# A four-layer graph attention stack: weight loads on GpSimd's queue, weight products moved, and other DMA latencies in the plan

## Chip, cores and metric

The kernel runs on one core of one Trainium2 chip. The metric is the device time of one execution in microseconds (us). A core has TensorE (PE: matmuls into PSUM; its weight loads are listed apart as PEld), VectorE (DVE), ScalarE (ACT), GpSimd (POOL) and SyncE (SP), which here does nothing but issue DMAs. ScalarE and GpSimd can issue DMAs too.

## The reference

128 graphs of 128 nodes with 512 features pass four layers. Each layer is a graph attention with a residual and a layer norm:

```python
x = _layernorm(x + _L0_gnn_ref(x, adj, ...))      # one head, no projection, bias b0
x = _layernorm(x + _L1_gnn_ref(adj, x, ...))      # two GAT layers: 4 heads of 256 (elu), then one of 512
x = _layernorm(x + _L2_gnn_ref(x, adj, W, a1, a2))  # 8 heads of 64
x = _layernorm(x + _L3_gnn_ref(x, adj, W_fc, W_attn))  # one head, scores from W_fc, elu
```

Every attention is of one form: two scores per node (source and target) are added over all pairs, go through a leaky relu with slope 0.2, are masked by the adjacency, and a softmax of them mixes the node features. Scores are products of projected features and attention vectors, so `x @ W @ a`; all is float32.

## The kernel before

**One graph.** A graph is one tile of 128 nodes by 512 features. The function `graph(g)` lists its operations in the order of the layers, each with an engine and a cost in us that the author gave it. The pieces that return:

- `score` (L491): products of the features with a score vector on VectorE (layers 0 and 3).
- `spread` (L326 to L333): turns a score column into a row. VectorE transposes it, one DMA on SP writes it to DRAM (`row<-sT`), a second reads it back to all 128 partitions (`w<-row`). This pair of DMAs is the "spread pair"; `nh` is the number of heads.
- `attend`: leaky relu on ScalarE (L383), mask and row minimum on VectorE (L391), exponential on ScalarE (L400), reciprocal of the sum (L408), then `turned`.
- `turned` (L344 to L359): transposes a tile of 128 x 128n. VectorE transposes blocks of 32, a DMA on SP writes them to DRAM (`scr<-w`, L349), a second reads them back (`w<-scr`, L359, or L354 where `moving` is set). This is the "turned pair".
- `project` (L449): the matmuls with the layer's weights. w1a (four chunks deep, 1032 columns in three parts), w2a (eight deep, 514 columns in two parts), wha (four deep, 528 columns in two parts).
- `mixed` (L466), `block` (L536) and `heads` (L581): the attention's matmul with the features.
- `norm`: statistics on VectorE (L418, L419), the inverse root on GpSimd (L422, L423), the scaling on VectorE (L435) or ScalarE (L431).

From its input to its output, a graph goes through one input DMA and then twelve pairs one after the other: spread and turned in layer 0, turned for x1, spread and turned in the first half of layer 1, spread and turned in the second half, turned for x2, spread and turned in layer 2, spread and turned in layer 3. GpSimd also makes the masks (L477, L480).

**The plan.** `Pipeline.plan` takes the operations of one graph and gives each a time, with every engine's time taken modulo `PERIOD`. It picks the next operation by its ready time, less `URGENCY` times the longest way to the end, plus a random shift of up to `SPREAD` (from `SEED`). `LATENCY` has two numbers for each engine: what passes from the end of an operation until a later one on the same engine, or on another, may use the result. An operation's `extra` is added to it. Graph g gets these times plus g times `PERIOD`. `run` sorts all operations of all graphs by time and emits them in that order. On the chip the times mean nothing any more: every engine works through its own list in this order and starts each operation as soon as its data is there.

**The setup.** The weights and the products that are made of them are entered into the same sorted list by `at(t, ...)`, with a time t in us of the plan:

- `weights`, `rows` and `passing` load weights with DMAs from `nc.scalar` (L213, L222).
- The score columns of a projection are appended to its weights: w1a times the attention vectors a1 in 32 products (`dot`, L262), w2a times a2 in 16 (L262), wha times a3 in eight pairs of a product and a reduction (`dots`, L280 and L281). `columns` (L294) makes the two score vectors wf of layer 3.
- A buffer of `passing` has a time until which its slot is kept.

Of the kernel before, what the change touches and what calls it, by code (L numbers as in the profile page):

```python
# [16 lines left out]
P = 128  # L17
# [7 lines left out]

PERIOD = 24.4
LATENCY = {"PE": (0.0, 0.8), "DVE": (0.15, 1.4), "ACT": (0.1, 1.4), "POOL": (0.1, 1.4), "SP": (9.0, 9.0)}
URGENCY = 1.0  # L30
BANKS = 8

SEED, SPREAD = 67, 3.0


class Buf:
# [30 lines left out]
class Pipeline:  # L67
# [3 lines left out]
    def plan(self, ops):  # L71
# [28 lines left out]
        while waiting:  # L100
# [4 lines left out]
            while True:  # L105
                u = t % PERIOD
                clash = [
                    y + d - u for x, y in spans for d in (-PERIOD, 0.0, PERIOD)
                    if u < y + d - 1e-9 and x + d < u + op.cost - 1e-9
# [3 lines left out]
                t += min(clash) + 1e-9  # L113
                assert t < ready[k] + 2 * PERIOD, "the period is too short"
            spans.append((t % PERIOD, t % PERIOD + op.cost))
            times[k] = t
# [7 lines left out]
    def run(self, setup):  # L124
# [8 lines left out]
        for g, ops in enumerate(graphs):  # L133
            alive = dict(zip(dict.fromkeys(b for op in ops for b in op.bufs), names))
            for k, op in enumerate(ops):
                events.append((g * PERIOD + times[k], g, k, op))
                op.ends = [(b, g * PERIOD + until[alive[b]]) for b in op.outs]
        for t, g, k, op in sorted(events, key=lambda e: e[:3]):
# [12 lines left out]
def tile_gat_stack(  # L151
# [25 lines left out]
    nc = tc.nc  # L177
    B, N, F = x.shape
    H1, FH = a1_src.shape
    HF = H1 * FH  # L180
    H2, FO = ah1.shape
    KF = F // P
    KH = HF // P
    OUT = w_fc.shape[0]
# [21 lines left out]
    def at(t, emit, bufs=()):  # L206
        setup.append((t, emit, bufs))

    def weights(t, shape, name, *loads, step=0.0):

        tl = const.tile(shape, F32, name=name)
        for n, (part, src) in enumerate(loads):
            at(t + n * step, lambda part=part, src=src: nc.scalar.dma_start(out=part(tl), in_=src))  # L213
        return tl

    def rows(t, ap, n, name):
        return weights(t, [P, n], name, (lambda w: w, ap.partition_broadcast(P)))

    def passing(t, until, n, src=None):

        b = Buf("setup", [P, n])
        load = lambda: nc.scalar.dma_start(out=b.ap[: src.shape[0]], in_=src)  # L222
        at(t, load if src is not None else lambda: None, [(b, until)])
        return b

# [1 line left out]

    C1, C2, C3 = HF + 2 * H1, F + 2, F + 2 * H2
    flat = "h f -> (h f)"
    w0d = rows(-20, w0_dst, F, "w0d")  # L230
    w0s = rows(-20, w0_src, F, "w0s")
    b0t = rows(-20, b0, 1, "b0t")
    a1 = [passing(-20, 40, HF, a.rearrange(flat).partition_broadcast(P)) for a in (a1_src, a1_dst)]

    w1a = weights(-20, [P, KF, C1], "w1a", *(
        (lambda w, b=b: w[b::4, :, :HF], w1.rearrange("(k b a) c -> b a k c", b=4, a=32)[b])
        for b in range(4)
    ))
    b1t = weights(-20, [P, KH], "b1t", (lambda w: w, b1.rearrange("(k p) -> p k", p=P)))
    b2t = rows(-20, b2, F, "b2t")  # L240
    a2 = [passing(-20, 110, F, a.rearrange(flat).partition_broadcast(P)) for a in (a2_src, a2_dst)]
    w2a = weights(-20, [P, KH, C2], "w2a", (lambda w: w[:, :, :F], w2.rearrange("(k p) c -> p k c", p=P)))
    fc = passing(20, 220, F, w_fc)
    ac = weights(20, [OUT, 2], "ac", *(
        (lambda w, s=s: w[:, s : s + 1], w_attn[0:1, s * OUT : (s + 1) * OUT].rearrange("u o -> o u"))
        for s in range(2)
    ))
    a3 = [passing(20, 180, F, a.rearrange(flat).partition_broadcast(P)) for a in (ah2, ah1)]
    wha = weights(40, [P, KF, C3], "wha", *(
        (lambda w, b=b, k=k: w[b::4, k, :F].rearrange("p (h o) -> p h o", h=H2),  # L250
         wh.rearrange("h (k b a) o -> b k a h o", b=4, a=32)[b, k])
        for k in range(KF) for b in range(4)
    ), step=1.2)
    acb = [passing(190, 220, P) for _ in range(2)]
    wf = const.tile([P, 2, F], F32, name="wf")
    prod = [passing(-20, 180, F) for _ in range(2)]
    turn = [0]

    def dot(w, a, out):

        turn[0] ^= 1
        nc.vector.tensor_tensor_reduce(  # L262
            out=prod[turn[0]].ap[:, : a.shape[1]], in0=w, in1=a, scale=1.0, scalar=0.0, op0=ALU.mult,
            op1=ALU.add, accum_out=out,
        )

    for k in range(KF):
        for s in range(2):
            for h in range(H1):
                c, o = slice(h * FH, (h + 1) * FH), HF + s * H1 + h  # L270
                at(14 + 4 * k + 2 * s + h / 2, lambda k=k, s=s, c=c, o=o: dot(w1a[:, k, c], a1[s].ap[:, c], w1a[:, k, o : o + 1]))
    for k in range(KH):
        for s in range(2):
            at(84 + 2 * k + s, lambda k=k, s=s: dot(w2a[:, k, :F], a2[s].ap, w2a[:, k, F + s : F + s + 1]))

    def dots(k, s):

        turn[0] ^= 1
        pr = prod[turn[0]].ap
        nc.vector.tensor_mul(pr, wha[:, k, :F], a3[s].ap)  # L280
        nc.vector.tensor_reduce(  # L281
            out=wha[:, k, F + s * H2 : F + (s + 1) * H2], in_=pr.rearrange("p (h o) -> p h o", h=H2),
            op=ALU.add, axis=AX.X,
        )

    for k in range(KF):
        for s in range(2):
            at(150 + 3 * k + 1.5 * s, lambda k=k, s=s: dots(k, s))

    def columns(s):  # L290

        nc.vector.tensor_copy(acb[s].ap[:OUT], ac[:, s : s + 1].to_broadcast([OUT, P]))
        pf = psum.tile([P, 512], F32, tag="ps7", name=f"pf_{s}")
        nc.tensor.matmul(pf, lhsT=acb[s].ap[:OUT], rhs=fc.ap[:OUT], start=True, stop=True)  # L294
        nc.vector.tensor_copy(wf[:, s, :], pf)

    for s in range(2):
        at(200 + 3 * s, lambda s=s: columns(s))

    work = ctx.enter_context(tc.tile_pool(name="work", bufs=1))  # L300
    dram = ctx.enter_context(tc.tile_pool(name="dram", bufs=1, space=bass.MemoryType.DRAM))
# [8 lines left out]
    def graph(g):  # L310
# [11 lines left out]
        def spread(col, nh):  # L322


            sT, row = Buf(f"sT{nh}", [P, nh, 32]), Buf(f"row{nh}", [nh, P])
            op("DVE", 0.12 + 0.033 * nh, lambda: nc.vector.transpose(  # L326
                sT.ap, col().unsqueeze(2).to_broadcast([P, nh, 32])
            ), [col.buf], [sT])
            op("SP", 0.6, lambda: nc.sync.dma_start(
                out=row.ap.rearrange("h (b c) -> b h c", b=P // 32), in_=sT.ap[0:P:32]  # L330
            ), [sT], [row])
            db = Buf(f"db{nh}", [P, nh, P])
            op("SP", 0.4, lambda: nc.sync.dma_start(  # L333
                out=db.ap.rearrange("p h j -> p (h j)"),
                in_=row.ap.rearrange("h j -> (h j)").partition_broadcast(P),
            ), [row], [db], 0.2 * nh)
            return db

        def turned(src, n, moving=False):

            zb, scr, out = Buf(f"zb{n}", [P, 4, n, 32]), Buf(f"scr{n}", [P, n * P]), Buf(f"pt{n}", [P, n, P])
            op("DVE", 0.12 + 0.133 * n, lambda: nc.vector.transpose(  # L344
                zb.ap.rearrange("p b h c -> p h b c"),
                src.ap.rearrange("p (h b c) -> p h b c", h=n, c=32) if len(src.shape) == 2
                else src.ap.rearrange("p h (b c) -> p h b c", c=32),
            ), [src], [zb])
            op("SP", 0.4, lambda: nc.sync.dma_start(  # L349
                out=scr.ap, in_=zb.ap.rearrange("p b h c -> p (b h c)")  # L350
            ), [zb], [scr], 0.2 * n)
            flat = lambda: scr.ap.rearrange("p f -> (p f)")
            if moving:
                op("SP", 0.6, lambda: nc.sync.dma_start(  # L354
                    out=out.ap.rearrange("p h i -> p (h i)").rearrange("p (q e) -> p q e", q=4),
                    in_=flat().rearrange("(q p e) -> p q e", q=4, p=P),
                ), [scr], [out], 0.2 * n)
                return out
            op("SP", 0.65, lambda: nc.sync.dma_start(  # L359
                out=out.ap.rearrange("p h (q c) -> p h q c", q=4),  # L360
                in_=flat().rearrange("(q p h c) -> p h q c", q=4, p=P, h=n),
            ), [scr], [out], 0.3 * n)
            return out

        class Col:
# [106 lines left out]
        x0, at = Buf("x0", [P, F]), Buf("adj", [P, P], I32)  # L472
# [25 lines left out]
        db = spread(Col(sc0, 1, 1), 1)  # L498
# [23 lines left out]
        db = spread(Col(xl, HF, H1), H1)  # L522
# [38 lines left out]
        db = spread(Col(xl2, F, 1), 1)  # L561
# [10 lines left out]
        db = spread(Col(xl3, F, H2), H2)  # L572
        x3 = Buf("x3", [P, F])

        def heads(q):
# [25 lines left out]
        db = spread(Col(sc4, 1, 1), 1)  # L601
# [6 lines left out]
            out=y.ap, in0=e3.ap, scalar=-1.0, in1=r3.ap, op0=ALU.add, op1=ALU.min  # L608
# [43 lines left out]
```

## Time and profile before

| what | value |
| --- | --- |
| median of 3 runs | 3224.28 us (3223.27 to 3225.53) |
| the profiled execution | 3223.46 us, span 3221.70 us |
| PE busy | 3081.6 us (96%), 14212 matmuls |
| PEld busy | 2375.8 us (74%) |
| DVE busy | 2792.0 us (87%) |
| ACT busy | 2470.8 us (77%) |
| POOL busy | 1545.5 us (48%) |
| DMA | 600.51 MB, mean 186 GB/s; SP's queue 588.39 MB, ACT's 8.20 MB |
| mean granted TensorE clock | 0.983 |

The profile is of one execution. Its span goes from the first to the last instruction of the program; the execution's own time lies 1.76 us above it. Busy time counts overlapping instructions of an engine once. Matmuls are pipelined, and each float32 matmul of the program shows as two records. A name such as `w<-scr` means that the tile on the left was written from the one on the right; buffer numbers are left out. The views name instructions by the line of the kernel (L449) and say what ended the idle time before them. SPq and ACTq stand for the instructions with which these engines issue DMAs.

### The profile page before, as it was taken

How to read it: one execution, taken by the hardware profiler on the slowest of the kernel's cores; microseconds unless marked ns; L12 is line 12 of the kernel's file. 1: busy time of each engine (PE TensorE's matmuls, PEld its weight loads, DVE VectorE, ACT ScalarE, POOL GpSimd, SP SyncE). 2: the span in 40 equal slices, each digit the busy share in tenths (PEclk: the TensorE clock that was granted, in tenths of full speed). 3: DMA queues.
4: the chain of work that ended last, by engine and by line, in shares of the span. 5: the costliest groups of instructions: out<-in, count | busy, mean ns of one | idle time of the engine just before them, and what ended most of it. 6: DMA issues, size and time to landing. Idle time of an engine off the chain costs nothing.

```text
span 3221.7 us, 61247 instructions
## 1 busy us (share of the span) xinstructions
PE 3081.6 (96%) x14212; PEld 2375.8 (74%) x14212; DVE 2792.0 (87%) x9976; ACT 2470.8 (77%) x8961; POOL 1545.5 (48%) x2310
## 2 busy tenths in 40 slices
PE   3799999999999999999999999999999999999974
PEld 1577777777777777777777777777777777777752
DVE  5567899999998999989999899898999989998786
ACT  0457888788787887878878888788887888878875
POOL 2234454554545545455454554545545455454334
PEclk9899999999999999999999999999999999999995
DMA  5357888888888888888888888888888888888675
GB/s 157 95 128 182 188 194 200 188 201 193 195 199 189 200 194 195 199 189 201 194 193 201 189 199 195 191 202 189 198 196 193 200 189 197 198 192 194 166 166 127
DMA packets 1641212, 600.51 MB, mean 186 GB/s; under 512 B 1310449, under 2 KB 1490673, under 8 KB 1640849
## 3 DMA queue, kind: packets, MB, share of 16 engines
q1 hardware_dynamic: 1632256, 588.39, 77.8%
q10 hardware_dynamic: 8592, 8.20, 0.8%
q8 instruction: 115, 1.88, 0.3%
q14 instruction: 249, 2.03, 0.2%
HBM read 368.91 MB, written 227.48 MB: 185 GB/s over the span
## 4 chain that ended last, share of the span: by engine, by line
PE 93%; DVE 2%; DMA 2%; ACT 2%; issue 1%; POOL 0%; ACTq 0%; SPq 0%; POOLq 0%; DVEq 0%
PE ps L449 69%; PE ps L466 10%; PE ps L536 7%; PE ps L581 6%; ACT w L400 1%; DMA w<-row 0%; PE ps L502 0%; DMA w<-scr 0%; ACT w L545 0%; DVE w L391 0%; DMA w<-in_x_dram 0%; ACT w L383 0%; DMA w_-1_2_96<-in_L_gnn_att_dst_dram 0%; DVE w L491 0%; DVE w_-1_4_110 L262 0%
## 5 line engine op out<-in xcount | busy, mean ns | idle before, releaser
L449 PE MATMUL ps<-w1a,w 128*128 128x344 f32 x3072 | 919.8, 456 | 14.0 <-DVE w L509 9.1
L449 PE MATMUL ps<-w2a,w 128*128 128x257 f32 x4096 | 917.6, 381 | 1.1 <-ACT xl L457 1.1
L400 ACT ACTIVATE w<-w,nm 128x128 f32<-128x128 f32 x1920 | 746.3, 415 | 144.3 <-DVE nm L391 142.4
L449 PEld LDWEIGHTS ps<-w2a,w 128*128 128x128 f32 x4096 | 765.8, 189 | 112.1 <-ACT xl L457 3.2
L449 PEld LDWEIGHTS ps<-w1a,w 128*128 128x128 f32 x3072 | 587.7, 192 | 307.8 <-DVE w L509 10.6
L545 ACT ACTIVATE w<-ps,b1t 128x128 f32<-128x128 f32 x2048 | 573.7, 386 | 49.5 <-PE ps L536 49.5
L383 ACT ACTIVATE w<-w,xl 128x128 f32<-128x128 f32 x1664 | 541.8, 395 | 84.8 <-PE ps L466 60.6
L422 POOL TENSOR_SCALAR rd<-mv 128x1 f32<-128x1 f32 x512 | 154.5, 302 | 935.8 <-DVE mv L419 918.8
L391 DVE CUSTOM_DVE_ANT_0 w<-w,w 128x128 f32<-128x128 f32 x1920 | 586.6, 395 | 15.6 <-ACT w L383 12.1
L344 DVE STREAM_TRANSPOSE w<-w 128x512 f32<-128x512 f32 (+1 forms) x1024 | 553.4, 546 | 10.4 <-ACT w L400 6.9
L457 ACT COPY xl<-ps 128x344 f32<-128x344 f32 (+2 forms) x640 | 265.8, 415 | 338.1 <-PE ps L449 320.5
L449 PE MATMUL ps<-wha,w 128*128 128x264 f32 x2048 | 503.3, 389 | 4.4 <-DMA w<-scr 4.4
L449 PEld LDWEIGHTS ps<-wha,w 128*128 128x128 f32 x2048 | 383.5, 192 | 122.0 <-issue 62.1
L400 ACT ACTIVATION_READ_ACCUMULATOR w<-w,nm 128x1 f32 x1920 | 410.4, 214 | 0.0
L418 DVE BATCH_NORM_STATS2 st<-w 128x6 f32<-128x512 f32 x512 | 353.9, 691 | 9.6 <-POOL w L610 2.8
L423 POOL TENSOR_TENSOR rd<-rd,neghalf 128x1 f32<-128x1 f32 x512 | 289.4, 565 | 42.7
L466 PE MATMUL ps<-w,w 128*128 128x512 f32 x512 | 260.8, 627 | 44.2 <-DMA w<-scr 23.0
L581 PEld LDWEIGHTS ps<-xl,w 128*128 128x128 f32 x2048 | 272.0, 195 | 37.6 <-ACT w L605 15.3
L391 DVE DVE_READ_ACCUMULATOR2_ANT nm<- 128x1 f32 x1920 | 290.5, 151 | 0.0
L491 DVE CUSTOM_DVE_ANT_0 w<-w,wf 128x512 f32<-128x512 f32 x256 | 284.5, 1146 | 4.4
L610 POOL TENSOR_TENSOR w<-w,w 128x512 f32<-128x512 f32 x128 | 184.1, 1439 | 202.9 <-issue 165.4
L581 PE MATMUL ps<-xl,w 128*128 128x64 f32 x2048 | 261.3, 272 | 17.5 <-ACT w L605 12.1
(63 smaller groups left out, 3741.0 us busy)
## 6 DMA issues: line engine op xcount, KB each, us to landing
scr<-w SPq DMA_DIRECT2D x640, 256.0 KB
w<-scr SPq DMA_DIRECT2D x640, 256.0 KB
w<-row SPq DMA_DIRECT2D x128, 512.0 KB
w<-in_x_dram SPq DMA_DIRECT2D x128, 256.0 KB
w<-row SPq DMA_DIRECT2D x128, 256.0 KB
out_dram<-w SPq DMA_DIRECT2D x128, 256.0 KB
w<-row SPq DMA_DIRECT2D x384, 64.0 KB
scr<-w SPq DMA_DIRECT2D x384, 64.0 KB
```

Of the source, the lines that this page charges most:

```text
L344: op("DVE", 0.12 + 0.133 * n, lambda: nc.vector.transpose(zb.ap.rearrange("p b h c -> p h b c"), src.ap.rearrange("p (h b c) -> p h b c", ...
L383: nc.scalar.activation(z.ap[:, h, :], db.ap[:, h0 + h, :], AF.Prelu, bias=src(h0 + h), alpha=SLOPE)
L391: nc.vector.tensor_tensor_reduce(out=zz.ap[:, h, :].rearrange("p (b a) -> p a b", b=4), in0=z.ap[:, h, :].rearrange("p (a b) -> p a b", b= ...
L400: nc.scalar.activation(zz.ap[:, h, :], zz.ap[:, h, :], AF.Exp, bias=nm.ap[:, h : h + 1], scale=-1.0, accum_out=rs.ap[:, h : h + 1],)
L418: op("DVE", 0.6, lambda: nc.vector.bn_stats(st.ap, y.ap), [y], [st])
L423: nc.gpsimd.tensor_tensor(out=rd.ap, in0=rd.ap, in1=neghalf, op=ALU.pow)
L449: op("PE", w * 4 / 2400 + 0.006, lambda k=k: nc.tensor.matmul(px.ap[:, :w], lhsT=xT.ap[:, k, :], rhs=wa[:, k, cols], start=(k == 0), stop= ...
L457: op("ACT", 0.16 + w / 1200, lambda: nc.scalar.copy(t.ap[:, cols], px.ap[:, :w]), [px], [t])
L466: op("PE", width * 4 / 2400, lambda: nc.tensor.matmul(pa.ap[:, :width], lhsT=pt.ap[:, 0, :], rhs=xv.ap[:, :width], start=True, stop=True), ...
L491: op("DVE", 0.75, lambda: nc.vector.tensor_tensor_reduce(out=jk.ap, in0=xv.ap, in1=wv, scale=1.0, scalar=init, op0=ALU.mult, op1=ALU.add, ...
L545: nc.scalar.activation(out.ap[:, k, :], pa.ap[:, u * P : (u + 1) * P], func, bias=b1t[:, k : k + 1])
L581: op("PE", 0.225, lambda u=u, h=h: nc.tensor.matmul(pa.ap[:, u * FO : (u + 1) * FO], lhsT=pt.ap[:, u, :], rhs=xl3.ap[:, h * FO : (h + 1) * ...
```

## The change

The loads of most weights go from ScalarE's queue to GpSimd's; w0d, w0s, b0t and b1t stay on ScalarE's; the 16 loads of wha go to SP's queue, 4 us of the plan apart. w2a is loaded in four DMAs, not one. The times of the loads and of the weight products in the plan change, and so do the times for which passing buffers are kept. SP's latency in the plan goes from 9.0 to 6.0 us, and the extras of the DMAs from 0.2nh, 0.2n and 0.3n to 1.0 + 0.1nh, 1.0 and 1.5 (the reloads); that of the input and of the store to `scr` stay. `PERIOD`, `URGENCY`, `SEED` and `SPREAD` have other values.

```diff
-PERIOD = 24.4
-LATENCY = {"PE": (0.0, 0.8), "DVE": (0.15, 1.4), "ACT": (0.1, 1.4), "POOL": (0.1, 1.4), "SP": (9.0, 9.0)}
-URGENCY = 1.0
+PERIOD = 24.7
+LATENCY = {"PE": (0.0, 0.8), "DVE": (0.15, 1.4), "ACT": (0.1, 1.4), "POOL": (0.1, 1.4), "SP": (6.0, 6.0)}
+URGENCY = 0.6
 BANKS = 8
-SEED, SPREAD = 67, 3.0
+SEED, SPREAD = 62, 8.0
...
-    def weights(t, shape, name, *loads, step=0.0):
+    def weights(t, shape, name, *loads, step=0.0, by=nc.gpsimd):
...
-            at(t + n * step, lambda part=part, src=src: nc.scalar.dma_start(out=part(tl), in_=src))
+            at(t + n * step, lambda part=part, src=src: by.dma_start(out=part(tl), in_=src))
...
-        load = lambda: nc.scalar.dma_start(out=b.ap[: src.shape[0]], in_=src)
+        load = lambda: nc.gpsimd.dma_start(out=b.ap[: src.shape[0]], in_=src)
...
-    w0d = rows(-20, w0_dst, F, "w0d")
-    w0s = rows(-20, w0_src, F, "w0s")
-    b0t = rows(-20, b0, 1, "b0t")
-    a1 = [passing(-20, 40, HF, a.rearrange(flat).partition_broadcast(P)) for a in (a1_src, a1_dst)]
-    w1a = weights(-20, [P, KF, C1], "w1a", *(
+    w0d = rows(-20, w0_dst, F, "w0d", nc.scalar)
+    w0s = rows(-20, w0_src, F, "w0s", nc.scalar)
+    b0t = rows(-20, b0, 1, "b0t", nc.scalar)
+    w1a = weights(-19, [P, KF, C1], "w1a", *(
...
-    b1t = weights(-20, [P, KH], "b1t", (lambda w: w, b1.rearrange("(k p) -> p k", p=P)))
-    b2t = rows(-20, b2, F, "b2t")
-    a2 = [passing(-20, 110, F, a.rearrange(flat).partition_broadcast(P)) for a in (a2_src, a2_dst)]
-    w2a = weights(-20, [P, KH, C2], "w2a", (lambda w: w[:, :, :F], w2.rearrange("(k p) c -> p k c", p=P)))
-    fc = passing(20, 220, F, w_fc)
-    ac = weights(20, [OUT, 2], "ac", *(
+    a1 = [passing(-18, 90, HF, a.rearrange(flat).partition_broadcast(P)) for a in (a1_src, a1_dst)]
+    b1t = weights(-18, [P, KH], "b1t", (lambda w: w, b1.rearrange("(k p) -> p k", p=P)), by=nc.scalar)
+    b2t = rows(16, b2, F, "b2t")
+    w2a = weights(18, [P, KH, C2], "w2a", *(
+        (lambda w, k=k: w[:, k : k + 2, :F], w2[k * P : (k + 2) * P].rearrange("(k p) c -> p k c", p=P))
+        for k in range(0, KH, 2)
+    ))
+    a2 = [passing(20, 130, F, a.rearrange(flat).partition_broadcast(P)) for a in (a2_src, a2_dst)]
+    a3 = [passing(60, 230, F, a.rearrange(flat).partition_broadcast(P)) for a in (ah2, ah1)]
+    fc = passing(60, 270, F, w_fc)
+    ac = weights(60, [OUT, 2], "ac", *(
...
-    a3 = [passing(20, 180, F, a.rearrange(flat).partition_broadcast(P)) for a in (ah2, ah1)]
-    wha = weights(40, [P, KF, C3], "wha", *(
+    wha = weights(70, [P, KF, C3], "wha", *(
...
-    ), step=1.2)
+    ), step=4, by=nc.sync)
...
-                at(14 + 4 * k + 2 * s + h / 2, lambda k=k, s=s, c=c, o=o: dot(w1a[:, k, c], ...))
+                at((31, 33, 56, 58)[k] + s + h / 4, lambda k=k, s=s, c=c, o=o: dot(w1a[:, k, c], ...))
...
-            at(84 + 2 * k + s, lambda k=k, s=s: dot(w2a[:, k, :F], ...))
+            at(100 + 3 * k + 1.5 * s, lambda k=k, s=s: dot(w2a[:, k, :F], ...))
...
-            at(150 + 3 * k + 1.5 * s, lambda k=k, s=s: dots(k, s))
+            at(190 + 6 * k + 3 * s, lambda k=k, s=s: dots(k, s))
...
-        at(200 + 3 * s, lambda s=s: columns(s))
+        at(250 + 3 * s, lambda s=s: columns(s))
...
-            ), [row], [db], 0.2 * nh)
+            ), [row], [db], 1.0 + 0.1 * nh)
...
-                ), [scr], [out], 0.2 * n)
+                ), [scr], [out], 1.0)
...
-            ), [scr], [out], 0.3 * n)
+            ), [scr], [out], 1.5)
```

More of the change, by code (lines that the diff above doesn't have):

```diff
@@ L207, in at, with rows @@
         setup.append((t, emit, bufs))
[L209 removed]
+    def weights(t, shape, name, *loads, step=0.0, by=nc.gpsimd):
         tl = const.tile(shape, F32, name=name)
         for n, (part, src) in enumerate(loads):
[L213 removed]
+            at(t + n * step, lambda part=part, src=src: by.dma_start(out=part(tl), in_=src))
         return tl
[L216 to L217 removed]
+    def rows(t, ap, n, name, by=nc.gpsimd):
+        return weights(t, [P, n], name, (lambda w: w, ap.partition_broadcast(P)), by=by)
     def passing(t, until, n, src=None):
         b = Buf("setup", [P, n])
[L222 removed]
+        load = lambda: nc.gpsimd.dma_start(out=b.ap[: src.shape[0]], in_=src)
         at(t, load if src is not None else lambda: None, [(b, until)])
@@ L252, in tile_gat_stack @@
         for k in range(KF) for b in range(4)
-    ), step=1.2)
-    acb = [passing(190, 220, P) for _ in range(2)]
+    ), step=4, by=nc.sync)
+    acb = [passing(240, 270, P) for _ in range(2)]
     wf = const.tile([P, 2, F], F32, name="wf")
-    prod = [passing(-20, 180, F) for _ in range(2)]
+    prod = [passing(-20, 230, F) for _ in range(2)]
     turn = [0]
@@ L270, in tile_gat_stack @@
                 c, o = slice(h * FH, (h + 1) * FH), HF + s * H1 + h
-                at(14 + 4 * k + 2 * s + h / 2, lambda k=k, s=s, c=c, o=o: dot(w1a[:, k, c], a1[s].ap[:, c], w1a[:, k, o : o + 1]))
+                at((31, 33, 56, 58)[k] + s + h / 4, lambda k=k, s=s, c=c, o=o: dot(w1a[:, k, c], a1[s].ap[:, c], w1a[:, k, o : o + 1]))
     for k in range(KH):
         for s in range(2):
-            at(84 + 2 * k + s, lambda k=k, s=s: dot(w2a[:, k, :F], a2[s].ap, w2a[:, k, F + s : F + s + 1]))
+            at(100 + 3 * k + 1.5 * s, lambda k=k, s=s: dot(w2a[:, k, :F], a2[s].ap, w2a[:, k, F + s : F + s + 1]))
     def dots(k, s):
```

## The prediction

> **What bounds the kernel now.** I read the page's slices first, then the busy time by stretches, then the chain, then the timeline of the first 60 us.
>
> ```profile
> PE   3799999999999999999999999999999999999974
> PEclk9899999999999999999999999999999999999995
> ```
>
> TensorE is full in all slices but the first two and last two. The stretches give it exactly (columns: length, then busy us and count for PE, PEld, DVE, ACT, POOL, then clock, DMA share, GB/s):
>
> ```profile
> 0.00:60.00 60.00, 8.20 (x11) 2.73 (x12) 29.20 (x127) 3.97 (x10) 14.74 (x26) 1.00 0.61 176
> 60.00:100.00 40.00, 30.74 (x78) 17.17 (x76) 23.20 (x74) 10.37 (x34) 13.51 (x19) 0.87 0.39 98
> 100.00:150.00 50.00, 40.19 (x158) 28.25 (x159) 30.62 (x88) 21.11 (x81) 14.38 (x20) 0.86 0.35 86
> 400.00:3000.00 2600.00, 2600.00 (x12176) 2020.96 (x12175) 2354.69 (x8434) 2111.12 (x7676) 1322.19 (x1970) 1.00 0.83 195
> 3100.00:3150.00 50.00, 31.30 (x130) 21.58 (x130) 45.93 (x162) 35.65 (x121) 20.15 (x33) 0.87 0.81 191
> ```
>
> From 400 to 3000 TensorE never stops. The chain shows its period:
>
> ```profile
> 360.86 9.61 PE ps L449 x36
> ...
> 384.55 9.61 PE ps L449 x36
> ...
> 408.25 9.61 PE ps L449 x36
> ```
>
> One graph costs 23.70 us of TensorE; 128 cost 3033.6. The profiled execution took 3223.46 (span 3221.70 plus 1.76 around it; 0.82 under the median of 3224.28). So 188 us of the span are TensorE time lost, all at the two ends. I weigh every matmul record by what it takes when TensorE is full (0.29 us w1a, 0.217 w2a, 0.223 wha, 0.43 mixed, 0.11 the small ones, scaled to 23.70 a graph) and subtract the sum from the clock: lost are 57.0 us before 60, 17.2 to 100, 15.7 to 150, 1.9 to 200, nothing up to 3000; then 4.9 to 3050, 10.8 to 3100, 25.6 to 3150, 35.3 to 3200 and 20 to the end. **Head 92, tail 96.**
>
> Where the head goes:
>
> ```profile
> 15.64 0.43 DVE L262 CUSTOM_DVE_ANT_0 w_-1_4_110<-w1a,w_-1_1_94 128x256 f32<-128x256 f32 x1 [6.80 <-DMA w1a<-in_L_gnn_W_dram]
> ...
> 28.74 0.33 DVE L391 CUSTOM_DVE_ANT_0 w<-w,w 128x128 f32<-128x128 f32 x1
> ```
>
> VectorE runs the 32 w1a products (11.7 us, 15.6 to 27.3) ahead of graph 0's first mask (L391), which then starts at 28.74. ScalarE, whose queue issues all weight loads, is no better:
>
> ```profile
> 20.89 0.59 ACTq L222 DMA_DIRECT2D w_-1_7_154<-in_L_gnn_a_dram  x1
> 21.51 1.28 ACT L383 ACT_TABLE_LOAD   x1 [21.51 <-DMA w_-1_2_106<-in_L_gnn_att_dst_dram]
> ```
>
> It starts its first activation only after 19 issues. Later it stands for 16 wha issues (29.1 to 41.0, 0.62 each), as its next activation shows:
>
> ```profile
> 40.39 0.40 ACT L383 ACTIVATE w<-w,sc 128x128 f32<-128x128 f32 x1 [10.79 <-DMA wha<-in_L_gnn_W_dram]
> ```
>
> The first w1a matmul is late:
>
> ```profile
> 56.97 1.51 PE L449 MATMUL ps<-w1a,w 128*128 128x344 f32 x2 [1.97 <-DVE w L509]
> ```
>
> **What the Trainium skill says.** *DMA: Bandwidth & Descriptors*, "Issuing engines are not separate DMA queues": transfers of all queues share 16 engines, a second queue saves only issue time. Agreed, but here the issue time is the cost: 0.62 us a piece, in front of waiting activations. The same page, "Anatomy of one DMA": a DMA issued by GpSimd has about 2.0 us of fixed cost. *SBUF — State Buffer*, "A bandwidth-pool intuition that's wrong": such a DMA of 620 ns took 3100 beside a VectorE copy that locked GpSimd out. No GpSimd-issued DMA is in the trace of before, so these two are prices only.
>
> **The change, part by part.**
>
> *1. w1a products to 31-35 and 56-60 of the plan.* Graph 0 then has its mask before them. Its way to the first w1a matmul, with rows of the trace: the row's broadcast is issued at 12.43 and lands near 16.4 (landings in the head: 3.4 to 4.1 us); prelu 0.40, mask 0.45, exp 0.55, transpose 0.31, store 1.54 and reload 3.38, mixed matmul 2.05 (cold clock), residual 0.74, statistics 0.85, GpSimd root 0.80, scale 0.55, transpose 0.71, store 2.0, reload 3.7: 18.0, and some 2 for hand-overs, ends at 36.5. The products are 32 x 0.35 = 11 us still; 16 fall beside graph 0's first store and reload (4.9 us of flight), 16 beside its second (5.7 us). Up to 5.6 us can lie in front of a transpose. I take 40 for the first w1a matmul: **-17** (from -9 to -20).
>
> *2. Loads off ScalarE's queue.* Only w0d, w0s, b0t and b1t stay: 4 x 0.43. The table load and the 10.8 us stop are gone; both are inside the 17. The 16 wha loads go to SP, every 4 us of the plan: 16 x 0.62 = 10 us of SP issue. SP issues 29 DMAs a graph, 16.6 us of 23.7 with waits in the full stretch, far fewer in the head, when only the first layers run. Queued behind each is one graph transfer, 0.6 us later: at most 1-2 us on graph 0. I take nothing.
>
> *3. 18 issues on GpSimd.* Six stand before graph 0's masks (w1a x4, a1 x2), seven at 16-20, five at 60. GpSimd was free from 1.3 to 8.9 us in before. At 1 us each they are over by 7.3: hidden. At 2.0 by 13.3, masks by 15.5, needed at about 17: hidden still. At 3.1 by 20, masks at 22: +5. I take nothing; 5 goes to the range. The later ones are in front of a norm's root (L422), 0.8 us, or a mask; TensorE is not full then, so a delay of a few us is possible, in the same bound.
>
> *4. w2a and wha products later and further apart.* 16 x 0.69 = 11 us and 8 x (0.68 + 0.69) = 11 us. In before the wha products sit in the chain from 100.3 to 110.7, before L509 of graph 3, while TensorE is not full. At 190-238 of the plan (6 us apart for 2.7 us) they fall after it has filled, where VectorE has 9% spare. The w2a products stay in the half-filled part, but 1.5 us apart.
>
> *5. The plan's DMA latency, 9.0 to 6.0 with other extras.* It moves no work; it only sets each engine's order. A graph's chain has its input and twelve pairs of DMAs. By the plan's sums a spread pair shrinks by 5 + 0.1nh, a turned pair by 4.5 + 0.3n, the moving pair by 5.8, the input by 3: 9.9 (first layer) + 5.7 + 11.2 + 9.9 + 5.7 + 11.5 + 9.9 + 3 = **66.8 us less plan**, 18.6 of it before w1a, 48.2 after. In the full stretch a graph stands 482 us from input to output (graph 64: 1432.8 to 1915.0), 496 of plan; 429 at the new period of 24.7 are 412. So 17.4 graphs are in flight, not 20.3.
>
> Tail: the last graph's w1a starts at 3016.2, with 206 us to the end and 110 of TensorE work left (3033.6 less 3016 - 92); the loss, 96, is the difference. From w1a to output the spacing goes from 390 to 339 (x0.87). If both shrink so, 179 - 95 = 84: **-12** (0 to -30). Head: the way from first w1a to a full TensorE holds 35 lost us; without 10 of wha products and with x0.87, 22, plus some 5 for the denser w2a products and the wha issues: **-8** (0 to -13).
>
> *6. PERIOD, URGENCY, SEED, SPREAD.* These reshuffle the order. In the full stretch the plan has only to keep every hand-over later than its data. From the semaphore updates, landings between 400 and 2900 are 2.1 to 4.4 us in the median and 6.3 at most; the new plan allows 6.6 to 8.2. I keep 23.70.
>
> Sum: -17 - 8 - 12 = -37: 3223.5 - 37 = 3186.
>
> **The rivals.**
> *Only the head gains.* For: VectorE is 92% busy from 3100 to 3150, so the tail may be its backlog and not the depth. Against: the backlog is itself what is in flight. 3223 - 25 = 3199.
> *GpSimd's issues are slow.* At 3 us each masks and w1a come late: the first w1a near 50, head -7 -5, tail -12: 3200.
> *Slower: the full stretch no longer fits.* With 3 us less slack at each DMA, and a more random order, one hand-over each period comes late and TensorE waits for it in all 110 full periods. At 0.34 us a period the 37 are gone; at 0.5 it is +55 - 37: 3241. For: VectorE has 2.2 us spare in 23.7 and stands in a fixed order; its L551 takes 0.95 us where the plan has 0.6. Against: the old plan with the same price errors never waits, and no landing reaches the new allowance.
> *The plan does nothing to the depth*, since engines start as soon as they can: same as the first rival.
>
> **How the numbers follow.** The forecast gets 0.64, head only 0.14, slow GpSimd 0.12, slower 0.10. A loss in the full stretch of under 0.3 us a period still leaves it faster. 0.2% is 6.4 us, about what a measurement can tell from no change: faster 0.88, same 0.04, slower 0.08. Range: best 20 + 13 + 30 = 63 gives 3160, worst of the faster cases 9 + 0 + 0 gives 3214; I give 3157 to 3214.
>
> **What would show it.** Right: the first w1a matmul near 40; no ScalarE wait for wha; wha products after TensorE is full; w1a starts 23.70 apart; input to output near 412 in the full stretch; last w1a to end near 179. Wrong: a PE wait that repeats each period, a period of over 23.8, a depth still near 480, or GpSimd DMA rows of 2 us and more ahead of the first masks.

## The result and the profile after

The median went from 3223.78 us (3223.11 to 3225.53, 4 runs) to 3200.81 us (3195.65 to 3201.20, 4 runs): ratio 0.9924 [0.9907, 0.9941], 23 us less where 37 were forecast, and inside the forecast's range of 3157 to 3214. The profiled execution took 3201.2 us, span 3199.3. In the kernel after, the lines of the loads stand one higher (L214, L223) and those from the products on four: L453 is the old L449, L470 the old L466, L395 the old L391.

First the slices of TensorE and its clock, on the page of the kernel after:

```profile
PE   3999999999999999999999999999999999999974
PEclk9999999999999999999999999999999999999985
```

The second slice is full now (it was 7); the tail's digits are unchanged. The stretches of the kernel after (length, then busy us and count for PE, PEld, DVE, ACT, POOL, then clock, DMA share, GB/s):

```profile
0.00:60.00 60.00, 14.36 (x31) 6.96 (x31) 27.30 (x114) 5.08 (x13) 22.19 (x42) 1.00 0.53 167
60.00:100.00 40.00, 27.10 (x75) 15.69 (x76) 28.07 (x88) 14.66 (x54) 17.15 (x21) 0.81 0.50 117
100.00:150.00 50.00, 48.97 (x217) 37.12 (x217) 32.10 (x101) 27.11 (x103) 16.11 (x23) 0.98 0.38 102
400.00:2950.00 2550.00, 2550.00 (x11969) 1987.79 (x11968) 2517.27 (x8304) 2053.25 (x7546) 1304.42 (x1941) 1.00 0.79 196
3100.00:3150.00 50.00, 29.09 (x105) 21.31 (x103) 34.05 (x141) 31.52 (x111) 18.63 (x29) 0.69 0.73 164
```

TensorE is busy for 49 of the 50 us after 100, where it was for 40; before 60 it has 14 us, not 8. From 400 to 2950 it never stops, as before. From 3100 to 3150 it does no more than before (29.1 against 31.3). The chain of the kernel after shows the period:

```profile
361.22 9.97 PE ps L453 x38
...
384.87 9.97 PE ps L453 x38
```

384.87 less 361.22 is 23.65; over graphs 20 to 100 it is 23.645, against 23.697 before. With the accounting of the prediction (matmul records by what they take when TensorE is full, subtracted from the clock) the 23 us are:

| lost TensorE time, us | before | predicted | after |
| --- | --- | --- | --- |
| up to the first w1a matmul | 57.0 | 40 | 50.9 |
| from there to a full TensorE | 34.6 | 27 | 28.8 |
| full stretch, 400 to 3000, relative to 23.70 a graph | 0 | 0 | -5.8 |
| tail | 96.6 | 84 | 91.7 |
| sum of the changes | | -37 | -23 |

The first row is the time of that matmul; the 2.1 us of products that TensorE does before it, in both kernels, are taken off in the second row.

That 23 of the 37 came is in part luck: the first w1a matmul gained 6 and not 17, the tail 5 and not 12, and 6 us came from a place where nothing was forecast.

**The head.** The timeline of the kernel after (start, us, engine, line, operation; in brackets the idle time before it and what ended it):

```profile
1.28 0.78 POOL L214 DMA_DIRECT2D w1a<-in_L_gnn_W_dram  x1 [0.35 <-issue]
...
9.68 0.61 SPq L333 DMA_DIRECT2D row<-sT  x1
...
13.37 2.87 POOL L214 DMA_DIRECT2D w2a<-in_L_gnn_W_dram  x4
...
15.00 0.33 SPq L337 DMA_DIRECT2D w<-row  x1
...
21.56 1.28 ACT L387 ACT_TABLE_LOAD   x1 [21.56 <-DMA w<-row]
...
24.67 0.33 SPq L353 DMA_DIRECT2D scr<-w  x1
...
26.65 0.77 DVE L495 CUSTOM_DVE_ANT_0 w<-w,w0d 128x512 f32<-128x512 f32 x1
...
28.84 0.74 DVE L495 CUSTOM_DVE_ANT_0 w<-w,w0s,b0t 128x512 f32<-128x512 f32 x1
...
30.78 0.52 SPq L333 DMA_DIRECT2D row<-sT  x1
31.39 0.39 SPq L363 DMA_DIRECT2D w<-scr  x1
...
39.80 0.80 SPq L353 DMA_DIRECT2D scr<-w  x2
...
45.89 0.51 SPq L333 DMA_DIRECT2D row<-sT  x1
46.51 1.12 SPq L363 DMA_DIRECT2D w<-scr  x2
...
50.90 2.63 PE L453 MATMUL ps<-w1a,w 128*128 128x344 f32 x4 [0.26 <-DMA w<-scr]
```

Two things are to be seen.

- *A late and slow broadcast.* The row of graph 0 is broadcast from 15.00, where the prediction had 12.43, and lands at 21.49: 6.5 us beside the four w2a loads, which GpSimd issues at 13.4 to 16.2. The prediction had it land near 16.4.
- *SP standing in order.* Graph 0's store to `scr` (24.67) landed at 26.19 by its semaphore update, but its reload `w<-scr` is issued at 31.39. SP stood at the instruction ahead of it, `row<-sT` of graph 1, which waits for graph 1's score; and that score's two products on VectorE (L495, 26.65 and 28.84) are interleaved with w1a products. The same happens again: the stores of 39.80 landed at 42.28 at the latest, the pair of reloads is issued from 46.51, behind another graph's `row<-sT` at 45.89. Graph 0's is the second of the pair.

The path of the prediction ended at 36.5. Put in the broadcast, 5.1 us late, and the two stands of SP, 5.2 and 4.2: 51.0. Measured: 50.9. That it fits so closely is chance in part: the table load (1.28 us from 21.56) also lies on the path, and the first reload took 1.94 us (31.39 to 33.33) where the path had 3.38.

### The profile page after: what moved, and what is told of

Read it like the earlier page. It is cut to its first block, busy times and chain, and to the rows that moved or that the text cites. A ratio compares the mean times of both kernels' runs of the same rounds, so it can differ in the third digit from the quotient of the medians.

```text
span 3199.3 us, 60449 instructions
## 1 busy us (share of the span) xinstructions
PE 3073.7 (96%) x14212; PEld 2378.0 (74%) x14212; DVE 3003.9 (94%) x9976; ACT 2444.6 (76%) x8961; POOL 1563.7 (49%) x2328
## 4 chain that ended last, share of the span: by engine, by line
PE 93%; DVE 3%; DMA 2%; POOL 1%; ACT 1%; issue 1%; SPq 0%; ACTq 0%; POOLq 0%; DVEq 0%
PE ps L453 69%; PE ps L470 10%; PE ps L540 7%; PE ps L585 6%; DMA w<-scr 1%; DVE w L495 0%; PE ps L506 0%; DMA scr<-w 0%; ACT w L404 0%; DVE w L395 0%; DVE st L422 0%; DMA w_-1_4_139<-in_L_gnn_att_dst_dram 0%; POOL rd L427 0%; DVE w L348 0%; DVE w_-1_1_94 L266 0%
## 5 line engine op out<-in xcount | busy, mean ns | idle before, releaser
L453 PE MATMUL ps<-w2a,w 128*128 128x257 f32 x4096 | 953.2, 380 | 3.1 <-DVE xl L458 3.1
L453 PE MATMUL ps<-w1a,w 128*128 128x344 f32 x3072 | 917.2, 455 | 1.9 <-ACT w L549 0.9
L453 PEld LDWEIGHTS ps<-w2a,w 128*128 128x128 f32 x4096 | 758.3, 190 | 121.1 <-DVE xl L458 3.9
L453 PEld LDWEIGHTS ps<-w1a,w 128*128 128x128 f32 x3072 | 587.4, 191 | 348.6 <-issue 41.1
L404 ACT ACTIVATE w<-w,nm 128x128 f32<-128x128 f32 x1920 | 767.3, 412 | 31.9 <-DVE nm L395 26.6
L395 DVE CUSTOM_DVE_ANT_0 w<-w,w 128x128 f32<-128x128 f32 x1920 | 666.3, 456 | 24.7 <-ACT w L387 11.6
L426 POOL TENSOR_SCALAR rd<-mv 128x1 f32<-128x1 f32 x512 | 118.5, 232 | 920.5 <-DVE mv L423 894.3
L453 PEld LDWEIGHTS ps<-wha,w 128*128 128x128 f32 x2048 | 390.4, 191 | 121.4 <-issue 36.8
L453 PE MATMUL ps<-wha,w 128*128 128x264 f32 x2048 | 480.0, 388 | 0.0
L523 POOL TENSOR_TENSOR w<-w,b2t 128x512 f32<-128x512 f32 x128 | 165.9, 1296 | 467.5 <-DVE w L348 282.0
L585 PEld LDWEIGHTS ps<-xl,w 128*128 128x128 f32 x2048 | 295.3, 197 | 104.2 <-issue 78.9
L427 POOL TENSOR_TENSOR rd<-rd,neghalf 128x1 f32<-128x1 f32 x512 | 307.4, 600 | 42.7
L470 PE MATMUL ps<-w,w 128*128 128x512 f32 x512 | 281.7, 633 | 32.5 <-DMA w<-scr 16.1
L585 PE MATMUL ps<-xl,w 128*128 128x64 f32 x2048 | 278.5, 271 | 25.4 <-DVE mv L423 9.9
L395 DVE DVE_READ_ACCUMULATOR2_ANT nm<- 128x1 f32 x1920 | 291.4, 152 | 0.0
L495 DVE CUSTOM_DVE_ANT_0 w<-w,wf 128x512 f32<-128x512 f32 x256 | 282.2, 1103 | 0.0
```

What stands on the lines that cost most here:

```text
L395: nc.vector.tensor_tensor_reduce(out=zz.ap[:, h, :].rearrange("p (b a) -> p a b", b=4), in0=z.ap[:, h, :].rearrange("p (a b) -> p a b", b= ...
L404: nc.scalar.activation(zz.ap[:, h, :], zz.ap[:, h, :], AF.Exp, bias=nm.ap[:, h : h + 1], scale=-1.0, accum_out=rs.ap[:, h : h + 1],)
L427: nc.gpsimd.tensor_tensor(out=rd.ap, in0=rd.ap, in1=neghalf, op=ALU.pow)
L453: op("PE", w * 4 / 2400 + 0.006, lambda k=k: nc.tensor.matmul(px.ap[:, :w], lhsT=xT.ap[:, k, :], rhs=wa[:, k, cols], start=(k == 0), stop= ...
L470: op("PE", width * 4 / 2400, lambda: nc.tensor.matmul(pa.ap[:, :width], lhsT=pt.ap[:, 0, :], rhs=xv.ap[:, :width], start=True, stop=True), ...
L495: op("DVE", 0.75, lambda: nc.vector.tensor_tensor_reduce(out=jk.ap, in0=xv.ap, in1=wv, scale=1.0, scalar=init, op0=ALU.mult, op1=ALU.add, ...
```

## The experiments

All times are medians beside fresh runs of the kernel before (3222.87 to 3223.8). The runs of one kernel lie up to 6 us apart in the kernel after and 8 in e5_deep_plan, so where times differ by less, the two traces are compared. Each trace is of one execution. *First w1a* is the time of the first w1a matmul; *head lost* and *tail lost* are the lost TensorE time before 400 us and after 3000.

| run | edit | us | ratio | first w1a | head lost | tail lost | period | depth |
| --- | --- | --- | --- | --- | --- | --- | --- | --- |
| before | | 3224 | | 57.0 | 91.6 | 96.6 | 23.697 | 482 |
| after | | 3201 | 0.9924 | 50.9 | 79.7 | 91.7 | 23.645 | 434 |
| e1_setup_only | old plan | 3212 | 0.9964 [0.9952, 0.9977] | 47.7 | 79.9 | 97.0 | 23.697 | 482 |
| e2_plan_only | old setup | 3195 | 0.9914 [0.9899, 0.9929] | 46.8 | 74.3 | 89.7 | 23.645 | 434 |
| e3_dots_early | w1a products early | 3194 | 0.9908 [0.9893, 0.9923] | 43.9 | 73.2 | 91.3 | 23.645 | 433 |
| e4_w2a_late | w2a loads late | 3205 | 0.9941 [0.9926, 0.9956] | 54.1 | 82.7 | 90.2 | 23.645 | 434 |
| e7_spread | both, w2a in pieces | 3190 | 0.9900 [0.9885, 0.9915] | 40.2 | 67.3 | 91.7 | 23.645 | 434 |
| e8_act_queue | ScalarE's queue | 3200 | 0.9929 [0.9914, 0.9944] | 51.5 | 77.0 | 90.6 | 23.645 | 433 |
| e5_deep_plan | seed 5 | 3203 | 0.9943 [0.9927, 0.9960] | 50.2 | 81.7 | 90.0 | 23.647 | 471 |
| f3_lat6_other | seed 39 | 3202 | 0.9933 [0.9917, 0.9950] | 49.3 | 76.8 | 94.6 | 23.648 | 450 |
| e6_lat5 | latency 5.0, seed 46 | 3225 | 1.0006 [0.9998, 1.0015] | 45.0 | 80.2 | 112.9 | 23.647 | 399 |
| f1_lat5_other | latency 5.0, seed 49 | 3211 | 0.9962 [0.9949, 0.9975] | 45.5 | 79.5 | 96.1 | 23.695 | 409 |
| f2_old_other | before with seed 4 | 3213 | 0.9967 [0.9954, 0.9980] | 57.1 | 88.7 | 87.4 | 23.696 | 515 |

Edits are against the kernel after, except the last. *Depth* is a graph's time from input to output in the full stretch, measured on graph 64.

### Setup alone, plan alone

The kernel after with the old `PERIOD`, `LATENCY`, `URGENCY`, `SEED`, `SPREAD` and extras:

```diff
-PERIOD = 24.7
+PERIOD = 24.4
...
-LATENCY = {..., "SP": (6.0, 6.0)}
+LATENCY = {..., "SP": (9.0, 9.0)}
```

> The kernel before with only the setup part of the change: loads on GpSimd's and SP's queues, and the new times of loads and products; the old plan (PERIOD 24.4, SP latency 9, old extras, seed 67). Theory A, the parts add up: the setup gives most of the head's gain. ScalarE no longer stands for the wha issues and the wha products leave the chain, so 8 to 12 us less, 3212 to 3216; the period stays at 23.70 and the input-to-output distance at 482 us. Theory B, the plan does all: the new setup's own delays (crowded transfers, products in front of SP's transfers) eat what it saves, 3220 to 3226.

And the kernel after with the old setup: loads on ScalarE's queue, the old times of loads and products.

```diff
-                at((31, 33, 56, 58)[k] + s + h / 4, lambda k=k, s=s, c=c, o=o: dot(w1a[:, k, c], ...))
+                at(14 + 4 * k + 2 * s + h / 2, lambda k=k, s=s, c=c, o=o: dot(w1a[:, k, c], ...))
```

> The changed kernel with the old setup part: all weights on ScalarE's queue, w2a in one DMA, old times of loads and products; the new plan (PERIOD 24.7, SP latency 6, new extras, seed 62). Theory A: period 23.645 instead of 23.70 (-6), tail 91 to 92 instead of 96 (-5), head still 90 or so because the 32 w1a products and the wha issues stand ahead of graph 0: 3209 to 3213. Theory B: nearly the changed kernel's time, 3199 to 3203.

The setup alone is worth 11 us, all in the head: 9.3 up to the first w1a matmul, 2.4 from there to a full TensorE. Which of its parts (queues, load times, product times) gave them was not separated. The plan alone is worth 28, more than either theory said; in the traces it is 30: head 17, full stretch 5.6, tail 7. Whether the latency or the new order gave the head's 17 was not separated. Together setup and plan give 23, so some 17 of 40 are lost, nearly all in the head. The plan doesn't need the new setup; with it, the kernel is some 6 us slower than without. The timeline of the plan-only kernel shows why (here with the old line numbers):

```profile
18.23 0.39 ACTq L213 DMA_DIRECT2D w2a<-in_L_gnn_W_dram  x1
...
25.07 0.37 DVE L391 CUSTOM_DVE_ANT_0 w<-w,w 128x128 f32<-128x128 f32 x1
...
28.48 0.33 SPq L349 DMA_DIRECT2D scr<-w  x1
29.16 0.51 SPq L329 DMA_DIRECT2D row<-sT  x1
...
30.61 0.39 SPq L359 DMA_DIRECT2D w<-scr  x1
```

The w1a products (15.8 to 27) run while w2a is in flight, in one DMA (18.23 to 28.41) that is issued after the broadcast (12.52 to 16.01) has landed; no transfer of graph 0 flies beside it. The products do hold graph 0's mask until 25.07, 1.7 us later than in the kernel after, where the late broadcast held it until 23.4, and the last six of them then stand ahead of its transpose, so that its store goes 3.8 us later (28.48 against 24.67). But SP has no stand: the store landed at 30.60 and the reload goes at 30.61. In the new setup the products no longer delay graph 0's mask; they delay graph 1's score, and through SP graph 0's reloads, by 9.4 us in two stands. So far this is a reading of the trace; the next run tests it.

### The products early

If that is so, the new setup with the products in VectorE's wait for the late broadcast must lose SP's stands.

```diff
-                at((31, 33, 56, 58)[k] + s + h / 4, lambda k=k, s=s, c=c, o=o: dot(w1a[:, k, c], ...))
+                at((18, 20, 36, 38)[k] + s + h / 4, lambda k=k, s=s, c=c, o=o: dot(w1a[:, k, c], ...))
```

> The changed kernel, with the 32 w1a products at 18 to 22 and 36 to 40 of the plan instead of 31 to 35 and 56 to 60, so that the first 16 fall into the time in which VectorE waits for graph 0's broadcast (12.8 to 23.4 us) and the rest behind graph 1's scores. Theory C: the products cost TensorE time through SP's order: they delay graph 1's transpose, SP waits for it, and graph 0's reload stands behind that (scr stored at 24.7, reload issued only at 31.4; and 39.8 to 46.5). Then the first w1a matmul comes at 40 to 44 instead of 50.9, and the time is 3190 to 3195. Theory D: the first w1a matmul is late only because the transfers crowd: it stays within 2 us of 50.9 and the time within 2 us of 3200.

SP's queue in the timeline of this kernel:

```profile
24.84 0.33 SPq L353 DMA_DIRECT2D scr<-w  x1
26.28 0.52 SPq L333 DMA_DIRECT2D row<-sT  x1
27.26 0.39 SPq L363 DMA_DIRECT2D w<-scr  x1
...
36.81 0.80 SPq L353 DMA_DIRECT2D scr<-w  x2
38.76 0.52 SPq L333 DMA_DIRECT2D row<-sT  x1
39.38 1.11 SPq L363 DMA_DIRECT2D w<-scr  x2
...
43.92 6.33 PE L453 MATMUL ps<-w1a,w 128*128 128x344 f32 x14 [0.35 <-DMA w<-scr]
```

The reloads go within 0.1 us of the landing of the stores (27.24 and 39.29), and the first w1a matmul comes 7 us sooner, as the first theory had it. The broadcast still landed at 21.67. So the stands are shown to come from the place of the products, and losing them is worth 7 us.

### The w2a loads late

```diff
-    b2t = rows(16, b2, F, "b2t")
-    w2a = weights(18, [P, KH, C2], "w2a", *(
+    b2t = rows(40, b2, F, "b2t")
+    w2a = weights(41, [P, KH, C2], "w2a", *(
...
-    a2 = [passing(20, 130, F, ...) for a in (a2_src, a2_dst)]
+    a2 = [passing(42, 130, F, ...) for a in (a2_src, a2_dst)]
```

> The changed kernel, with b2t, w2a and a2 loaded at 40 to 42 of the plan instead of 16 to 20. Theory D (crowding): graph 0's broadcast, issued at 15.0 and landed at 21.5 beside the 2 MB of w2a, lands near 18.5; the first w1a matmul comes 3 us earlier, 3196 to 3198. Theory C (SP's order): the products still hold SP for graph 1's transpose, so that most of it is lost again: within 1.5 us of the changed kernel, 3199 to 3202.

The broadcast took from 14.69 to 17.94, so the loads had been what slowed it: 3.6 of the 5.1 us by which it was late. The other 1.5 remain, since it is still issued at 14.7 and not at 12.43. But the first w1a matmul came at 54.1, three later than after, and the time is above what either theory gave. The timeline of this kernel:

```profile
24.16 2.87 POOL L214 DMA_DIRECT2D w2a<-in_L_gnn_W_dram  x4
26.94 0.52 SPq L333 DMA_DIRECT2D row<-sT  x1
...
27.55 0.76 SPq L363 DMA_DIRECT2D w<-scr  x1
...
33.25 0.33 SPq L337 DMA_DIRECT2D w<-row  x1
```

Now graph 0's reload is in flight beside them. It was issued at 27.55 and landed at 36.52, 8.97 us, where the same transfer takes 1.94 in the kernel after. SP's stands are there too: that reload goes 4.9 us after the landing of its store, the second 4.2. The burst of 2 MB delayed the transfer of graph 0 that flew beside it, in both kernels; moving it chose which.

### Both, and the loads spread

Products early, w2a in four pieces 12 us of the plan apart, a2 after them.

```diff
-    b2t = rows(16, b2, F, "b2t")
-    w2a = weights(18, [P, KH, C2], "w2a", *(
+    b2t = rows(42, b2, F, "b2t")
+    w2a = weights(44, [P, KH, C2], "w2a", *(
...
-    ))
-    a2 = [passing(20, 130, F, ...) for a in (a2_src, a2_dst)]
+    ), step=12)
+    a2 = [passing(84, 130, F, ...) for a in (a2_src, a2_dst)]
...
-                at((31, 33, 56, 58)[k] + s + h / 4, lambda k=k, s=s, c=c, o=o: dot(w1a[:, k, c], ...))
+                at((18, 20, 36, 38)[k] + s + h / 4, lambda k=k, s=s, c=c, o=o: dot(w1a[:, k, c], ...))
```

> The changed kernel with the w1a products early (18 to 22 and 36 to 40 of the plan) and the four w2a loads apart (44, 56, 68, 80), b2t at 42, a2 at 84. Theory: a burst of loads delays whatever transfer of graph 0 flies beside it, by up to 5 us, wherever it is put; in pieces of 0.5 MB each delays one by 2 us at most, and the products no longer hold SP. First w1a matmul at 38 to 41, time 3187 to 3191. If only the products count, it stays at the 3194 of the run with early products alone.

```profile
14.72 0.33 SPq L337 DMA_DIRECT2D w<-row  x1
...
21.32 0.33 SPq L353 DMA_DIRECT2D scr<-w  x1
22.77 0.52 SPq L333 DMA_DIRECT2D row<-sT  x1
23.79 0.38 SPq L363 DMA_DIRECT2D w<-scr  x1
...
32.70 0.80 SPq L353 DMA_DIRECT2D scr<-w  x2
...
35.27 1.11 SPq L363 DMA_DIRECT2D w<-scr  x2
...
40.17 5.10 PE L453 MATMUL ps<-w1a,w 128*128 128x344 f32 x14
```

In its timeline the broadcast landed at 17.95, and graph 0's reloads landed 2.0 and 4.2 us after their issue (23.79, and 35.70 for the second of the pair). The first w1a matmul starts at 40.2, 3.7 us sooner than with the early products alone: the place that the prediction had given the change. At 3190.1 us it beats the kernel before by 33 us and the kernel after by 11; the plan alone, with the old setup, had 28 of these 33.

### The same loads on ScalarE's queue

All loads that went to GpSimd go to ScalarE's queue, at the new times; wha stays on SP.

```diff
-    def weights(t, shape, name, *loads, step=0.0, by=nc.gpsimd):
+    def weights(t, shape, name, *loads, step=0.0, by=nc.scalar):
...
-        load = lambda: nc.gpsimd.dma_start(out=b.ap[: src.shape[0]], in_=src)
+        load = lambda: nc.scalar.dma_start(out=b.ap[: src.shape[0]], in_=src)
```

> The changed kernel with every load that stands on GpSimd's queue issued by ScalarE instead, at the same times in the plan; wha stays on SP, products as changed. Theory G, GpSimd's queue itself costs: its issues are not held back, so 3 MB are in flight from 1.3 us on and b0t, row and broadcast of graph 0 land 1 to 2.5 us later each than before the change; on ScalarE's queue the issues come spaced and the first w1a matmul is 3 to 5 us earlier, 3195 to 3198. Rival, the queue does not matter, only the times of loads and products do: within 2 us of 3200.8.

3199.6 against 3200.8, first w1a at 51.5 against 50.9: no difference that can be told, as the rival had it. But in the timeline two differences cancel:

```profile
11.74 0.33 SPq L337 DMA_DIRECT2D w<-row  x1
...
18.90 2.14 ACTq L214 DMA_DIRECT2D w2a<-in_L_gnn_W_dram  x4
...
22.27 1.28 ACT L387 ACT_TABLE_LOAD   x1 [22.27 <-DMA b2t<-in_L_gnn_b_dram]
```

The row and the broadcast start sooner (7.60 and 11.74, since ScalarE spaces its w1a issues over 6.2 us), and the broadcast has landed at 17.38, 4.1 us sooner than in the kernel after. But ScalarE works through its own list too: the issues of b1t, b2t, w2a and a2 (17.40 to 22.24) stand ahead of graph 0's first activation, which starts 4.9 us after its row has landed. The w2a loads then meet graph 0's store, which took from 25.38 to 30.68. The Trainium skill, *DMA: Bandwidth & Descriptors*, "Issuing engines are not separate DMA queues", says that all queues end on the same 16 engines and that only issue time differs. This run agrees as far as it goes: the 4.9 us pass at ScalarE's issues. So the queue, the headline of the change, gained nothing at these load times; that it never matters is not shown.

### The tail: depth, latency or order

The prediction scaled the tail with the depth. Two seeds were taken for the depth they give, the other constants kept: a deep plan at latency 6.0, and a shallow one at 5.0.

```diff
-SEED, SPREAD = 62, 8.0
+SEED, SPREAD = 5, 8.0
```

> The changed kernel with SEED 5 instead of 62: the same latencies and setup, another order, whose plan is 499 us deep instead of 458 (the old plan: 506). Theory E, the tail goes with the plan's depth, not with the latency constants: the input-to-output distance in the full stretch goes from 433 to about 470 us, the tail from 92 to 96-100 lost us, the head stays near 80: 3204 to 3209. Theory F, the lower latencies themselves make the tail short, whatever the depth: 3198 to 3202.

```diff
-LATENCY = {..., "SP": (6.0, 6.0)}
+LATENCY = {..., "SP": (5.0, 5.0)}
...
-SEED, SPREAD = 62, 8.0
+SEED, SPREAD = 46, 8.0
```

> The changed kernel with SP's latency at 5.0 instead of 6.0 and SEED 46: a plan of 424 us instead of 458, first w1a at 65 of the plan instead of 72. Theory E: distance in the full stretch near 400 us, tail some 4 us shorter, head 2 to 4 us shorter: 3190 to 3196. Rival: the slack is used up. Median landings are up to 5.2 us and the worst 6.8, the plan now allows 5.6 to 7.2, so TensorE waits in the full stretch: the period rises over 23.70, 3205 or more.

With 37 us more depth the tail lost 90.0, slightly less than after; with 35 us less it lost 112.9. Both go against the depth theory. Nor does its rival for the second run hold, that the slack is used up in the full stretch: the period stays at 23.647. To see whether the latency or the order that came with it was at fault, the same latencies were run with other seeds: 5.0 with seed 49, the kernel before (9.0) with seed 4, 6.0 with seed 39.

> The changed kernel with SP's latency at 5.0 and SEED 49: a second order with the latency of the run that lost 114 us in the tail; its plan is 431 us deep. Theory H, the constant decides: with the transfers planned this close, TensorE meets each late transfer at the ends, so the tail loses over 105 us again and the time is 3215 to 3230. Theory I, the order decides: the tail falls somewhere between 88 and 105, 3193 to 3212.

> The kernel before with SEED 4 instead of 67: old latency of 9.0, old setup, a plan of 541 us instead of 506. If depth counted, the tail would lose 7% more than its 96 us, 103, and the time would be 3229 or more. Theory H: depth does not count, the tail stays at 94 to 100 and the time within 4 us of 3223. Theory I: the tail is anywhere from 85 to 110.

> The changed kernel with SEED 39 instead of 62: a third order at SP latency 6.0, a plan of 475 us. Theory H: tail 88 to 94 as in the other two orders at 6.0, 3198 to 3204. Theory I: the tail differs from theirs by over 6 us.

At one latency the tail is 112.9 or 96.1 (5.0), 91.7, 90.0 or 94.6 (6.0), 96.6 or 87.4 (9.0). The seed alone moves it by 17 us at 5.0 and by 9 at 9.0; at 6.0 the three orders lie within 4.6, closer than theory I asked. Sorted by depth, 399 to 515, the tails read 112.9, 96.1, 91.7, 94.6, 90.0, 96.6, 87.4; the deepest graph has the shortest tail. So neither constant sets the tail alone: the order of operations that the plan happens to draw moves it as much. Seven orders are too few to rule out that deeper plans tend to shorter tails. One part is visible in the worst one. In the chain of the kernel e6_lat5:

```profile
3077.00 6.05 DMA w<-scr
3083.09 3.01 PE ps L453 x6
...
3095.72 5.97 DMA w<-scr
3101.83 2.98 PE ps L453 x6
...
3115.30 5.01 DMA w<-scr
3120.45 2.98 PE ps L453 x6
```

Once every 18 to 20 us the chain runs through a reload of 5 to 6 us, straight into projections, for which TensorE waits. In the chain of the kernel after such reloads take 2.4 to 3.6. But TensorE's waits for reloads do not rank the seven orders (63 us from 3032 to 3200 in f1_lat5_other, with a tail of 96; 31 in f2_old_other with 87), so what makes an order good at the end stays open.

The period goes with the order too. Four plans have 23.645 to 23.648 and three 23.695 to 23.697, and the two with latency 5.0 fall on either side.

## Why the prediction was right or wrong

**Step 1, first w1a matmul at 40 (-17, from -9).** Wrong: 50.9, outside its range. What the path to 36.5 held was right within some 2 us: the spread kernel has no stand, its broadcast lands 1.5 us late, and its first w1a matmul comes at 40.2 where the path then gives 38.1. Two terms were missed. The line "the row's broadcast is issued at 12.43 and lands near 16.4" took both times from the kernel before, in which no 2 MB load was in flight beside it and ScalarE spaced the w1a loads. "16 fall beside graph 0's first store and reload" looked only at VectorE: the products don't stand in front of graph 0's transpose, they stand in front of graph 1's score, and SP, which works in order, holds graph 0's reload behind it. The prediction had asked what SP's queue would do behind the wha issues and not behind a `row<-sT` that comes late.

**Step 2, nothing for 16 wha issues on SP.** Holds in the kernel after: ScalarE waits for no wha issue, and the first two start at 49.0, behind the last reload that the first w1a matmul needs. In e1_setup_only two stand ahead of and between reloads (40.88 and 42.21), at 0.6 us each, as priced. But the table load is not gone, as the step had it: its 1.28 us now start when the broadcast has landed (21.56), on graph 0's way.

**Step 3, GpSimd's issues hidden.** Right, and cheaper than any of its prices: 0.50 to 0.78 us each (w2a: 2.87 for four), against 1 to 3.1. The first six are over at 5.2. The rival "GpSimd's issues are slow" gave 50 for the first w1a matmul and 3200, which is what came out, but not by its mechanism: no mask waited for an issue. The 2.0 us that the Trainium skill gives in *DMA: Bandwidth & Descriptors*, "Anatomy of one DMA", should not have been a price of issue at all: by that section they are mostly the wait for the data to be confirmed as landed. From issue to landing the w1a pieces took 7.2 to 8.9 us, beside each other, so no run here shows the 2.0 alone.

**Step 4, wha and w2a products out of the way, -8 in the stretch to full (with step 5).** The size is near, -6, but the reason is not borne out. The products did move: the w2a products now lie between 66.8 and 86, the wha products between 134 and 152, when TensorE is full, and lost time from 100 to 150 fell from 15.7 to 2.4 us, of which some came back before 100 (17.2 to 20.8 from 60 on, where the w2a products now are) and after 150 (1.9 to 5.8). But from the first w1a matmul to full the plan alone, whose wha products still run from 97 to 112, loses 27.5 us, less than the kernel after with 28.8; the setup alone, which moves the products, loses 32.2, against 34.6 before. So by these two runs at most 2.4 of the 6 us can be put down to the products, and with the new plan they show no gain.

**Step 5, depth 412 and the tail x0.87.** The depth is 434. In us of the plan that is 434 x 24.7 / 23.645 = 453, 43 less than 496 and not 67: the latencies in the plan do shrink as summed, but a third comes back, by this sum as waits for the engines in the new order, which the prediction left out. From the last graph's first w1a matmul to the end 191 us pass, not 179 (205.5 before). The tail's -12 measured -5, and the rule behind it does not hold: over seven orders the tail does not grow with the depth.

**Step 6, "I keep 23.70".** Wrong by 0.05 us a graph, which is 0.2% of a period and 5.8 us in all. The matmuls are the same; only their order differs. Added up from start to start over one graph of the full stretch, the 64-column matmuls of the heads take 0.053 us less than before, but the 128-column ones 0.060 more; what is left is in the w2a matmuls, 0.053 less (216.9 ns each on average, not 218.6). In f1_lat5_other and f2_old_other, with the longer period, it is the w1a matmuls that take more (291.5 against 289.2). Why stays open.

**The rivals.** *Only the head gains* (3199) is near in size, but tail and period gained as well. *The full stretch no longer fits* is refuted: landings go up to 6.8 us, and TensorE never waits between 400 and 2950. *The plan does nothing to the depth* is refuted too: 434 against 482.

## What to carry to other kernels

A DMA queue that is fed in a fixed order can hold a transfer that is ready behind one that isn't: when a filler moves on a compute engine, follow what it delays into the queue, and who stands behind that. A bulk load in flight beside a transfer of a latency chain cost the chain 3 to 7 us here, so spread it in pieces between the chain's transfers, and don't issue it from an engine that has work of the chain behind it. And when a change carries a new random order with it, run the old constants with another seed first: here a seed alone was worth 11 us for the kernel before, and 13 at latency 5.0.

## What the runs showed that was not expected

VectorE's busy time rose while the kernel got faster. The mask on the page of the kernel before, then the page of the kernel after:

```profile
L391 DVE CUSTOM_DVE_ANT_0 w<-w,w 128x128 f32<-128x128 f32 x1920 | 586.6, 395 | 15.6 <-ACT w L383 12.1
...
PE 3073.7 (96%) x14212; PEld 2378.0 (74%) x14212; DVE 3003.9 (94%) x9976; ACT 2444.6 (76%) x8961; POOL 1563.7 (49%) x2328
...
L395 DVE CUSTOM_DVE_ANT_0 w<-w,w 128x128 f32<-128x128 f32 x1920 | 666.3, 456 | 24.7 <-ACT w L387 11.6
```

94% against 87%, with the same 9976 instructions; the mask's mean went from 395 to 456 ns. With seed 49 (f1_lat5_other) it is 2673 us (83%). So the recorded time of the same instruction changes with the order around it, and a higher busy share of VectorE did not go with a slower kernel: TensorE never waits in the full stretch at 94%. What the added time is, the traces do not show.
